# Transposing tokens by DMA between partitions and VectorE in 32 by 32 blocks, in place of TensorE, in a three-part decoder layer

## The chip, the cores and the metric

The kernel runs on one core of a Trainium2 chip. The metric is device time in microseconds (us). All rows of the profile come from one profiled execution; the kernel was also timed in three runs. TensorE is called PE in the profile, its weight loads PEld, VectorE DVE, ScalarE ACT, GpSimd POOL, and SyncE, which issues most DMAs, SP.

## The reference

One decoder layer in float32 for 4 batches of 1024 tokens with 512 features: gated self attention, cross attention to a context of 1024 x 384, and a small feed-forward network (FFN), each behind a layer norm and a residual. Both attentions have 16 heads of 32.

```python
# self attention, x normalized first (xn = layernorm(x))
inner, outer, v = heads(xn @ Wi), heads(xn @ Wo), heads(xn @ Wv)
a = softmax(inner @ outer.T / sqrt(32)) * sigmoid(xn @ Wa + ba)[query] * sigmoid(xn @ We + be)[key]
a = a / (a.sum(-1) + 1e-8)
x = x + rotate_and_gain(a @ v) @ Wout
# cross attention
q, k, v = heads(layernorm(x) @ Wq + bq), heads(ctx @ Wk + bk), heads(ctx @ Wv + bv)
x = x + (softmax(clip(q @ k.T / sqrt(32))) @ v) @ Wo + bo
# FFN: 64 channels, each through its own network of 16 hidden units
s = layernorm(x) @ Win + bin
g = sum_h(relu(s[..., None] * W1 + b1) * W2) + b2
x = x + g @ Wout + bout
```

## The kernel before

All time goes to `moderate_path`; `general_path` behind it runs only if a flag finds extreme values, and does not run here.

**Tiling.** A tile of tokens is [128 partitions, 512]. Half a batch is 4 such tiles (`xt` of [128, 4, 512], index `t`), a batch has two halves `hf`. A projection contracts over features, so normalized tokens, which lie with tokens on partitions, must be turned so that features lie on partitions. `tr(hf, t)` in `pre` does that: four `nc.tensor.transpose` of 128x128 (line 354) into one PSUM bank and a copy back over the tokens (`evacuate`, line 254 on ACT once attention has begun, line 258 on VectorE before). The `tr(t)` of `post` does the same (line 688) for the FFN's input. After that, chunk `c` of the features is `xn[:, :, ts(c, P)]`: 4 runs of 128 columns.

**Matmuls.** `columns` (line 86) splits each matmul with 128 output partitions into four of 32, which run abreast. Every float32 matmul shows as two PE instructions, a transpose as one.

**Passes.** `u` counts eight passes: phase 0 (self attention) for batches 0 to 3, then phase 1 (cross attention and FFN) for batches 0 to 3. `attention(u, hf)` gives 32 steps, 4 head groups `g` by 8 key tiles `kt`. A step computes scores for four heads (line 494), exponentials on ACT into the `e` tiles (line 499, two of six buffers a step), sums of `e` over key tiles on VectorE (`es`, lines 505 and 507; in phase 0 also `eg`, lines 514 and 515), and the `av` matmuls of the step before (line 521). Phase 0 and the last pass give part of the sums to TensorE (`shared`, line 529); passes 4 to 6 have two `es` additions of 128x1024 a step. At the end of a head group the sums go through small DMAs and DRAM: `add_up` (one step later) sends `sum_d` and `cs`, `divide` (two steps later) `rec_d` and four `recb` broadcasts to 32 partitions each, `multiply` (two more steps) needs them (line 601).

**Work beside the steps.** `pre(u)` holds the preparation of a pass (loads `x` or `ctx`, layer norm `ln`, transposes `tr`, projections `k`, `q`, `v`, gates `g` and `gt`), `post(u, hf)` what follows attention: loads, the output projection `o`, and in phase 1 layer norm, transposes and `inputs` (`s`), the hidden units `h` and `out`. `beside(u, hf)` writes out by hand, as a list, which of these runs next to which half: the preparation of pass u+1 and the post of the half before. Each entry has a load in units (one unit is a group of four matmuls of 512 columns abreast; a projection of one head group or one tile is 4 units, 3 from the context, and items with load 0 run as they are reached). `run` spreads the list so that the units are used up evenly over the 32 steps; `weave` mixes light items into heavy ones in a fixed proportion. On PE, VectorE, ACT and GpSimd the order of the program is kept; SP's DMAs are put in order by the framework's scheduler, and go out as their buffers come free.

**Buffers.** Tokens, context and the FFN's input share a pool `p3` of three buffers (`tok`). PSUM has two banks for everything that is no score and no accumulator (`bank()`). In phase 0 `r2` is one buffer between GpSimd and a store.

Of the kernel before, what the change touches and what calls it, by code (L numbers as in the profile page):

```python
# [16 lines left out]
P = 128  # L17
# [21 lines left out]
MAGIC = 0x5F3759DF  # L39

# [22 lines left out]
def moderate_path(tc: tile.TileContext, a: dict, out: bass.AP, flag: bass.AP):  # L63
    nc = tc.nc
    x = a["x"]
    with ExitStack() as st:
# [15 lines left out]
        def columns(to, lhsT, rhs, **flags):  # L82

            for j in range(4):
                r = slice(j * DH, (j + 1) * DH)
                nc.tensor.matmul(to[r], lhsT=lhsT[:, r], rhs=rhs, **flags)  # L86
# [7 lines left out]
        rec_d = [dram.tile([HG, HALF], F32, tag=f"rec_{i}", name="rec_d") for i in range(4)]  # L94
        wout_d = dram.tile([P, NC, D], F32, name="wout_d")
# [16 lines left out]
        def load_w(which):  # L112
            w = wp.tile([P, NC, D], F32, tag="w", name="w")
            if which == "o0":
                nc.sync.dma_start(w, wout_d)
            else:
                src, n = W_IN[which]
                nc.sync.dma_start(w[:, 0:n, :], src.rearrange("(c p) f -> p c f", p=P))
            return w

        x0 = p3.tile([P, 4, D], F32, tag="tok", name="xin")
        nc.sync.dma_start(x0, x[0].rearrange("(t p) d -> p t d", p=P)[:, 0:4, :])
        wae = const.tile([P, NC, 2 * H], F32, name="wae")
        nc.scalar.dma_start(wae[:, :, 0:H], a["attn_Wa"].rearrange("(c p) h -> p c h", p=P))
        nc.scalar.dma_start(wae[:, :, H:], a["attn_We"].rearrange("(c p) h -> p c h", p=P))
# [88 lines left out]
        nc.gpsimd.dma_start(win, a["ffn_Win"].rearrange("(c p) m -> p c m", p=P))  # L214
# [63 lines left out]

        order = [(ph, b) for ph in range(2) for b in range(B)]
# [15 lines left out]
        def pre(u):  # L295
# [4 lines left out]
            def load_ctx(hf):  # L300
                def f():
                    t = p3.tile([P, NC, HALF], F32, tag="tok", name="ctxT")
                    nc.sync.dma_start(
                        t[:, 0:NCK, :],
                        a["ctxT"][b].rearrange("(c p) t -> p c t", p=P)[:, :, hf * HALF : (hf + 1) * HALF],
                    )
                    me["ctx", hf] = lambda c: t[:, c, :]
                    me["ctx", hf, "t"] = lambda c, i: t[:, c, ts(i, P)]
                return f

            def load_x(hf):
                def f():
                    if u == 0 and hf == 0:
                        xt = x0
                    else:
                        xt = p3.tile([P, 4, D], F32, tag="tok", name="xin")
# [8 lines left out]
            def ln(hf):  # L325
# [14 lines left out]
                def norm(t):  # L340
                    def f():
                        xt = me["xn", hf][:, t, :]
                        normalized(xt, xt, res["mv"], res["rs"], t)
                    return [(0, f)]

                return [stats(t) for t in range(4)] + [[(0, root)]] + [norm(t) for t in range(4)]

            def tr(hf, t):
                def f():

                    xn = me["xn", hf]
                    tp = bank()
                    for c in range(NC):
                        nc.tensor.transpose(tp[:, ts(c, P)], xn[:, t, ts(c, P)], ident)
                    evacuate(xn[:, t, :], tp)
                    me["in", hf] = lambda c: xn[:, :, ts(c, P)]
                    me["in", hf, "t"] = lambda c, i: xn[:, i, ts(c, P)]
                return f
# [99 lines left out]
            def trs(hf):  # L458
                return [[(1, tr(hf, t))] for t in range(4)]
# [165 lines left out]
        def post(u, hf):  # L625

            ph, b = order[u]
            me = S[u]
# [43 lines left out]
            def root():  # L672
                i = 2 * NS + b * NT + 4 * hf
                nc.gpsimd.tensor_copy(marks[:, i : i + 4], res["mv"][:, :, 1])
                res["rs"] = rsqrt(res["mv"], 4)
                res["xn"] = p3.tile([P, 4, D], F32, tag="tok", name="xn")

            def norm(t):
                def f():
                    normalized(res["xn"][:, t, :], res[t], res["mv"], res["rs"], t)  # L680
# [3 lines left out]
            def tr(t):  # L684
                def f():
                    tp = bank()
                    for c in range(NC):
                        nc.tensor.transpose(tp[:, ts(c, P)], res["xn"][:, t, ts(c, P)], ident)  # L688
                    evacuate(res["xn"][:, t, :], tp)
                return f  # L690

            def inputs():
                ss = bank()
                for c in range(NC):
                    for j in range(4):
# [3 lines left out]
                            rhs=res["xn"][:, 2 * k : 2 * k + 2, ts(c, P)],  # L699
# [41 lines left out]
            if ph == 0:  # L741
# [5 lines left out]
                "s": [[(1, tr(t))] for t in range(4)] + [[(2, inputs)]],  # L747
# [38 lines left out]
        def beside(u, hf):  # L786

            last = post(u, 0) if hf else post(u - 1, 1) if u else None
            if u + 1 == n:
                out = last["load"] + pause(16) + last["o"] + weave(last["ln"], pause(4)) + pause(4)  # L790
                return out + last["s"] + weave(last["h"], pause(14)) + pause(2) + last["out"]
            p = pres[u + 1]
            next_ = pres[u + 2] if u + 2 < B else None
            if u + 1 < B:
                if hf == 0:
                    out = p["tr"][0] + p["x"][1] + p["k"][0][0:1] + p["g"][0] + p["k"][0][1:] + p["gt"][0]
                    if last:
                        out = last["load"] + out + weave(p["ln"][1], last["o"])
                    else:
                        out = one(rotations) + one(fold_bv) + out + [rotate(c) for c in range(NC)] + p["ln"][1]  # L800
                        out += [[(4, fold_bv)]]
                    return out + p["v"][0][0:1] + p["tr"][1] + p["v"][0][1:3] + p["g"][1] + p["v"][0][3:] + p["gt"][1]
                out = p["k"][1] + last["load"] + p["v"][1] + last["o"]
                if next_:
                    out += next_["x"][0]
                out += p["q"][0] + (weave(next_["ln"][0], p["q"][1][0:3]) if next_ else p["q"][1][0:3])
# [4 lines left out]
                return out + p["q"][1][3:]  # L811
            if hf == 0:
                out = p["ctx"][0] + p["ctx"][1] + last["load"] + p["k"][0]
                if "s" not in last:
                    return out + p["v"][0] + last["o"] + p["k"][1]
                out += p["v"][0][0:1] + last["o"] + weave(last["ln"], p["v"][0][1:2]) + p["v"][0][2:3] + last["s"]
                return out + weave(last["h"], p["v"][0][3:] + p["k"][1][0:3]) + p["k"][1][3:] + last["out"]
            if "s" not in last:
                out = last["load"] + p["v"][1][0:2] + p["x"][0] + p["v"][1][2:]
                out += p["x"][1] + weave(p["ln"][0], last["o"][0:3]) + last["o"][3:] + p["tr"][0]  # L820
                return out + p["q"][0][0:1] + weave(p["ln"][1], p["q"][0][1:]) + p["tr"][1] + p["q"][1]
            out = p["x"][0] + last["load"] + p["v"][1][0:1] + weave(p["ln"][0], p["v"][1][1:3]) + p["v"][1][3:]
            out += p["x"][1] + p["tr"][0] + p["q"][0][0:1] + weave(p["ln"][1], last["o"])
            out += weave(last["ln"], p["q"][0][1:2]) + p["q"][0][2:3] + last["s"]
            return out + weave(last["h"], p["q"][0][3:] + p["tr"][1] + p["q"][1][0:3]) + p["q"][1][3:] + last["out"]
# [3 lines left out]
        first += weave(p["ln"][1], p["q"][0]) + p["gt"][0] + p["tr"][1] + p["v"][0] + p["k"][1] + one(load_wout)  # L829
        first += p["g"][1] + p["q"][1] + p["gt"][1] + pres[1]["x"][0] + weave(pres[1]["ln"][0], p["v"][1])  # L830
# [667 lines left out]
```

## Time and profile before

| | us |
|---|---|
| median of three timed runs | 2300.78 (2300.62 to 2300.97) |
| the profiled execution | 2299.8 |
| its span, first to last instruction | 2298.0 |
| TensorE's granted clock, mean | 0.99 |

By parts of the span: 0 to 110 us prepare pass 0; the sixteen halves follow, 131 and 152 us in turn in phase 0 (128 and 140 in pass 3), 118 to 123 and 137 in phase 1, 113 and 111 in the last pass; from 2227.5 the post of the last half runs alone (70.5 us). A row of the groups gives line, engine, operation, output and inputs, shapes, count, then busy time in us and the mean of one in ns, then the engine's idle time before these instructions and what ended it. A row of the timeline gives start and length of merged instructions. A row of the windows gives a stretch, its length, then the busy time of each engine with its instruction count, the granted clock, the DMA engines' busy share and the GB/s moved.

### The profile page before, as it was taken

To read this page: it belongs to the slowest core of one execution; us is meant where nothing else is said; L and a number is where in the kernel's file an instruction comes from. 1 tells how busy PE (TensorE), PEld (TensorE's weight loads), DVE (VectorE), ACT (ScalarE), POOL (GpSimd) and SP (SyncE) were. 2 spreads that over 40 slices of the span, in tenths; PEclk is the share of its full clock that TensorE was granted. 3 is DMA by queue.
4 is the path that set the end of the run, shared out by engine and by line. 5 is a ranking of instruction groups with operands and counts; after the bars stand their busy time and mean duration, and the time that the engine had idled before them with its cause. 6 is when DMAs were issued, how large, how long until landed. Compare 5 with 4: busy or idle time off the path is not lost. (4 is left out here: it accounts for less than half of the span.)

```text
span 2298.0 us, 52871 instructions
## 1 busy us (share of the span) xinstructions
PE 2228.1 (97%) x22738; PEld 584.5 (25%) x22738; DVE 1528.2 (67%) x2401; ACT 1274.2 (55%) x1562; POOL 136.3 (6%) x143
## 2 busy tenths in 40 slices
PE   7999999999999999999999999999999999999984
PEld 2322222222222222222222222222222222222221
DVE  4368566775667756566865668678776878655554
ACT  0055545555455554555556565757576665757561
POOL 3000021000000000000000001000010101000100
PEclk9999999999999999999999999999999999999996
DMA  5202032120311203212311311202111221101010
GB/s 147 77 25 67 27 106 63 27 72 27 103 58 41 59 26 99 58 40 90 101 33 44 97 54 39 71 30 93 39 48 61 66 84 30 61 12 49 11 52 22
DMA packets 104021, 132.64 MB, mean 58 GB/s; under 512 B 44912, under 2 KB 45552, under 8 KB 102624
## 3 DMA queue, kind: packets, MB, share of 16 engines
q1 hardware_dynamic: 100464, 128.12, 18.0%
q8 instruction: 180, 2.95, 0.5%
q0 software_dynamic: 2000, 0.98, 0.3%
q14 instruction: 65, 0.53, 0.1%
q10 hardware_dynamic: 1312, 0.07, 0.0%
HBM read 101.00 MB, written 28.08 MB: 56 GB/s over the span
## 5 line engine op out<-in xcount | busy, mean ns | idle before, releaser
L499 ACT ACTIVATE e<-s 128x1024 f32<-128x1024 f32 x1024 | 994.2, 1023 | 719.3 <-PE s L494 526.4
L507 DVE TENSOR_TENSOR es<-es,e 128x1024 f32<-128x1024 f32 x528 | 645.6, 1246 | 331.5 <-ACT e L499 330.3
L494 PE MATMUL s<-q,k 32*64 32x512 f32 x8192 | 615.8, 613 | 6.2 <-ACT e L499 5.3
L521 PE MATMUL av<-e,v 128*32 128x512 f32 x4096 | 552.8, 604 | 0.0
L86 PE MATMUL f<-xin,w 128*32 128x512 f32 x3072 | 359.9, 596 | 4.7 <-ACT xin L254 3.9
L515 DVE SCALAR_TENSOR_TENSOR eg<-e,sw,eg 128x512 f32<-128x512 f32 x448 | 322.6, 756 | 2.3
L505 DVE TENSOR_TENSOR es<-e 128x1024 f32<-128x1024 f32 x88 | 115.4, 1334 | 234.0 <-ACT e L499 219.4
L86 PE MATMUL f<-w,q 128*32 128x512 f32 x2048 | 245.3, 598 | 10.0 <-DVE q L601 10.0
L494 PEld LDWEIGHTS s<-q,k 32*64 32x64 f32 x8192 | 136.0, 129 | 428.1 <-ACT e L499 208.6
L521 PEld LDWEIGHTS av<-e,v 128*32 128x32 f32 x4096 | 88.3, 108 | 403.6 <-issue 401.5
L86 PEld LDWEIGHTS f<-xin,w 128*32 128x32 f32 x3072 | 100.4, 110 | 233.3 <-issue 220.8
L529 PE MATMUL sm<-e,sw 128*2 128x512 f32 x1024 | 134.2, 596 | 0.0
L86 PE MATMUL f<-w,xin 128*32 128x512 f32 x1024 | 118.5, 592 | 0.7 <-DVE q L258 0.6
L661 POOL TENSOR_TENSOR r<-res,bo_bc 128x512 f32<-128x512 f32 x32 | 44.9, 1403 | 1124.4 <-DVE res L657 977.4
L86 PEld LDWEIGHTS f<-w,q 128*32 128x32 f32 x2048 | 67.4, 111 | 166.5 <-issue 149.9
L712 ACT ACTIVATE hid<-sT,units 128x256 f32<-128x256 f32 x128 | 72.0, 606 | 49.2 <-DVE sT L703 45.7
L86 PE MATMUL f<-ctxT,w 128*32 128x512 f32 x768 | 92.3, 592 | 0.0
L86 PE MATMUL f<-w,ctxT 128*32 128x512 f32 x768 | 91.7, 592 | 0.0
L718 DVE SCALAR_TENSOR_TENSOR g<-hid,units,g 128x256 f32<-128x256 f32 x120 | 57.9, 483 | 19.3 <-ACT hid L712 11.1
L551 PE MATMUL sm<-es,ones 128*1 128x512 f32 x352 | 68.2, 591 | 0.7 <-ACT both L540 0.7
L601 DVE TENSOR_TENSOR q<-both,recb 128x512 f32<-128x512 f32 x64 | 44.0, 687 | 27.7 <-DMA recb<-rec_d 27.4
L657 DVE TENSOR_TENSOR res<-f,res 128x512 f32<-128x512 f32 x64 | 44.0, 687 | 25.5 <-PE f L86 25.4
(231 smaller groups left out, 1081.2 us busy)
## 6 DMA issues: line engine op xcount, KB each, us to landing
recb<-rec_d SPq DMA_DIRECT2D x256, 64.0 KB
w<-in_xattn_Wo SPq DMA_DIRECT2D x9, 1024.0 KB
xin<-in_x SPq DMA_DIRECT2D x8, 1024.0 KB
res<-in_x SPq DMA_DIRECT2D x32, 256.0 KB
w<-wout_d SPq DMA_DIRECT2D x8, 1024.0 KB
x_d<-res SPq DMA_DIRECT2D x32, 256.0 KB
x1b_d<-r SPq DMA_DIRECT2D x32, 256.0 KB
xin<-x_d SPq DMA_DIRECT2D x32, 256.0 KB
```

The lines of the kernel that those rows point to most:

```text
L86: nc.tensor.matmul(to[r], lhsT=lhsT[:, r], rhs=rhs, **flags)
L494: nc.tensor.matmul(s[m : m + 64, j, :], lhsT=k[r, g, kt * P + m : kt * P + m + 64], rhs=q[r, g, :], start=True, stop=True,)
L499: nc.scalar.activation(e, s, AF.Exp, scale=SCALE)
L505: nc.vector.tensor_tensor(me["es"][i], me["e", 0][i], es[i], ALU.add)
L507: nc.vector.tensor_tensor(me["es"][i], me["es"][i], es[i], ALU.add)
L515: nc.vector.scalar_tensor_tensor(eg, es[0][:, h, :], gate(kt), eg, ALU.mult, ALU.add)
L521: nc.tensor.matmul(av[r, :], lhsT=me["v"][:, kt, HG * g + h, :], rhs=es[h // 2][:, h % 2, :], start=(kt == 0), stop=(kt == NT - 1),)
L529: nc.tensor.matmul(sm[j * DH : j * DH + sums, :], lhsT=me["sw"][:, t, HG * g + 2 + h, :] if ph == 0 else ones, rhs=me["e", t][1][:, h, :], ...
L551: nc.tensor.matmul(sm[j * DH : j * DH + 1, :], lhsT=ones, rhs=e, start=True, stop=True)
L661: nc.gpsimd.tensor_tensor(r2, r, bo_bc, ALU.add)
L712: nc.scalar.activation(hid, res["s"], AF.Relu, bias=units[:, 1, h : h + 1], scale=units[:, 0, h : h + 1])
L718: nc.vector.scalar_tensor_tensor(res["g"], res["hid"], units[:, 2, h - 1 : h], res["g"], ALU.mult, ALU.add)
```

## The change

Most transposes leave TensorE. They are split in two: DMAs move 32-row groups of tokens between partitions, and VectorE transposes 32x32 blocks in place.

- `spread` (15 of the 16 token sets, after the last norm of a set): 16 SP DMAs from the tokens (`tok`) to a second buffer `xT`; features of quarter `q` land on partitions 32q to 32q+31. `blocks` then transposes each [128, 512] tile on VectorE. In chunk `c`, partition 32q + i now holds feature 128q + 32c + i, and the chunk's columns lie in runs of 32 (`chunk`).
- Weights are loaded so that their rows match (`by_quarters`: four DMAs to 32 partitions each, for `q0`, `k0`, `v0`, `q1`, the gates' `wae` and the FFN's `win`).
- Before the FFN (7 of 8 posts), each norm writes to the one buffer `r2`, a DMA stores it to DRAM (`rows_d`), and after the fourth, four DMAs read the rows back in the spread order; then `blocks`.
- The first token set and the last post, where nothing runs beside, use `across`: 16 matmuls per tile against the identity, each 32 output partitions wide, into the same layout.
- Of the three `tok` buffers one stays for tokens and the FFN's input; two are now `inT`, for `xT`, the context and the first token set.
- `tr` items no longer count as load, and the lists of `beside` and of the start are written out anew so that other items stand between a spread and its `blocks`.

```diff
+NB = 32
             for j in range(4):
                 r = slice(j * DH, (j + 1) * DH)
-                nc.tensor.matmul(to[r], lhsT=lhsT[:, r], rhs=rhs, **flags)
+                nc.tensor.matmul(to[r], lhsT=lhsT[:, j, :] if len(lhsT.shape) == 3 else lhsT[:, r], rhs=rhs, **flags)
+        def by_quarters(dma, to, w):
+            for q in range(NC):
+                dma(to[ts(q, NB)], w[ts(q, P)].rearrange("(c i) f -> i c f", i=NB))
+        rows_d = [dram.tile([4, P, D], F32, tag=f"rows_{i}", name="rows_d") for i in range(2)]
...
+        def spread(to, xt):
+            for q in range(NC):
+                for s in range(P // NB):
+                    nc.sync.dma_start(to[ts(q, NB), :, ts(s, P)], xt[ts(s, NB), :, ts(q, P)])
+        def blocks(xt, t):
+            nc.vector.transpose(xt[:, t, :], xt[:, t, :])
+        def across(xt, t):
+            tp = bank()
+            for c in range(NC):
+                for q in range(NC):
+                    nc.tensor.matmul(
+                        tp[ts(q, NB), ts(c, P)], lhsT=xt[:, t, q * P + c * NB : q * P + (c + 1) * NB], rhs=ident,
+                        start=True, stop=True,
+                    )
+            to = xt[:, t, :].rearrange("p (s c j) -> p c s j", c=NC, j=NB)
+            evacuate(to, tp.rearrange("p (c s j) -> p c s j", c=NC, j=NB))
+        def chunk(xt, c, t0=0, n=4):
+            return xt[:, t0 : t0 + n, :].rearrange("p t (s c j) -> p (t s) c j", c=NC, j=NB)[:, :, c, :]
...
# pre: load_ctx, load_x, norm, tr
-                    t = p3.tile([P, NC, HALF], F32, tag="tok", name="ctxT")
+                    t = p2.tile([P, NC, HALF], F32, tag="inT", name="ctxT")
-                        xt = p3.tile([P, 4, D], F32, tag="tok", name="xin")
+                        xt = p1.tile([P, 4, D], F32, tag="tok", name="xin")
                         normalized(xt, xt, res["mv"], res["rs"], t)
+                        if xt0(hf):
+                            return
+                        if t == 3:
+                            me["xT", hf] = p2.tile([P, 4, D], F32, tag="inT", name="xT")
+                            spread(me["xT", hf], me["xn", hf])
-                    xn = me["xn", hf]
-                    tp = bank()
-                    for c in range(NC):
-                        nc.tensor.transpose(tp[:, ts(c, P)], xn[:, t, ts(c, P)], ident)
-                    evacuate(xn[:, t, :], tp)
-                    me["in", hf] = lambda c: xn[:, :, ts(c, P)]
+                    if xt0(hf):
+                        xn = me["xn", hf]
+                        across(xn, t)
+                    else:
+                        xn = me["xT", hf]
+                        blocks(xn, t)
+                    me["in", hf] = lambda c: chunk(xn, c)
-                return [[(1, tr(hf, t))] for t in range(4)]
+                return [[(1 if xt0(hf) else 0, tr(hf, t))] for t in range(4)]
...
# post: norm, tr
-                    normalized(res["xn"][:, t, :], res[t], res["mv"], res["rs"], t)
+                    if last:
+                        normalized(res["xn"][:, t, :], res[t], res["mv"], res["rs"], t)
+                    else:
+                        r2 = p1.tile([P, D], F32, tag="r2", name="r2")
+                        normalized(r2, res[t], res["mv"], res["rs"], t)
+                        nc.sync.dma_start(rows_d[hf][t], r2)
+                        if t == 3:
+                            for q in range(NC):
+                                nc.sync.dma_start(
+                                    res["xn"][ts(q, NB)].rearrange("j t (s f) -> j (t s) f", f=P),
+                                    rows_d[hf].rearrange("t (s j) f -> j (t s) f", j=NB)[:, :, ts(q, P)],
+                                )
+                return lambda: (across if last else blocks)(res["xn"], t)
...
# beside, the last pass, then phase 0, then phase 1 (hf 0, hf 1)
-                return out + last["s"] + weave(last["h"], pause(14)) + pause(2) + last["out"]
+                out = last["load"] + pause(16) + last["o"] + weave(last["ln"], pause(4)) + pause(4) + last["tr"]
+                return out + pause(2) + last["s"] + weave(last["h"], pause(14)) + pause(2) + last["out"]
+                    return out + v[0][0:2] + tr[1] + v[0][2:3] + p["g"][1] + v[0][3:] + p["gt"][1]
+                out = next_["x"][0] + k[1] + last["load"] + v[1] + last["o"] + weave(next_["ln"][0], q[0])
+                out += q[1][0:3] + next_["tr"][0] + q[1][3:]
+                out += k[0][0:3] + v[0][0:1] + last["o"] + weave(last["ln"], v[0][1:2]) + v[0][2:3] + last["tr"]
+                return out + v[0][3:] + last["s"] + weave(last["h"], k[1]) + k[0][3:] + last["out"]
+            out = x[0] + last["load"] + v[1][0:1] + weave(ln[0], v[1][1:3]) + v[1][3:] + x[1] + last["o"][0:1] + tr[0]
+            out += weave(ln[1], last["o"][1:])
+            out += weave(last["ln"], q[0][0:1]) + q[0][1:2] + tr[1] + last["tr"] + q[0][2:3] + last["s"]
+            return out + weave(last["h"], q[0][3:] + q[1][0:3]) + q[1][3:] + last["out"]
```

## The prediction

> **What bounds the kernel now.** I read the page first, for engine totals and the chain of work that ended last.
>
> ```profile
> PE 2228.1 (97%) x22738; PEld 584.5 (25%) x22738; DVE 1528.2 (67%) x2401; ACT 1274.2 (55%) x1562; POOL 136.3 (6%) x143
> ...
> PE 43%; ACT 2%; DVE 2%; issue 1%; DMA 1%; SPq 0%; DVEq 0%; ACTq 0%
> ```
>
> TensorE works 97% of the span and leads the chain; ACT has room everywhere. VectorE's 67% is a mean over unlike stages, so I cut the span at the ends of the 32-step halves (the copies of line 538 mark them): a phase-0 half with `hf`=0, then phase 1's `hf`=1 and `hf`=0 halves, and a half of the last pass.
>
> ```profile
> core 0: us, PE busy (x) PEld busy (x) DVE busy (x) ACT busy (x) POOL busy (x), PEclk, DMA share, GB/s
> 677.30:808.40 131.10, 131.10 (x1406) 35.00 (x1410) 97.72 (x156) 75.02 (x91) 7.06 (x5) 1.00 0.18 56
> 1346.50:1483.50 137.00, 134.40 (x1376) 37.29 (x1372) 106.48 (x169) 87.28 (x114) 7.54 (x5) 1.00 0.17 53
> 1483.50:1606.80 123.30, 122.88 (x1276) 31.82 (x1272) 92.68 (x121) 82.96 (x106) 6.63 (x5) 1.00 0.19 62
> 2003.60:2116.40 112.80, 112.19 (x1100) 27.11 (x1097) 62.82 (x96) 76.78 (x96) 6.75 (x5) 1.00 0.11 32
> ```
>
> The first two columns are the length and PE's busy time: PE is the limit in every half, at full clock (1.00). DVE comes nearest in phase 1's `hf`=1 (106.5 of 137).
>
> **What is removed.** 16 x 4 transposed tiles before projections and 8 x 4 before the FFN; tile sets (u=0, hf=0) and the last post stay on TensorE, so 60 + 28 = 88 tiles of four transposes go. Groups by line, then PE's timeline:
>
> ```profile
> L354 PE MATMUL f<-ident,xin 128*128 128x128 f32 x256 | 39.6, 293 | 17.0 <-DVE xin L277 13.4 <-ACT xin L254 2.6 <-DVE q L258 0.6
> L277 DVE TENSOR_SCALAR xin<-xin,bnmv,yi 128x512 f32<-128x512 f32 x64 | 32.8, 542 | 0.6
> L254 ACT COPY xin<-f 128x512 f32<-128x512 f32 x56 | 31.7, 596 | 6.4 <-PE f L354 6.4
> ```
> ```profile
> 1946.46 1.07 PE L521 MATMUL av<-e,v 128*32 128x512 f32 x8
> 1947.46 1.09 PE L688 MATMUL f<-ident,xn 128*128 128x128 f32 x8
> 1948.48 1.11 PE L494 MATMUL s<-q,k 32*64 32x512 f32 x16
> ```
>
> Where no transpose follows, the next group starts 0.88 us after `av` (1896.17 to 1897.05), so PE is free at 1947.34 and the next scores start at 1948.48: eight transposes hold it 1.14 us, a tile 0.57 us. 88 x 0.57 = 50 us. PE's idle time inside the halves is about 13 us (2.6 in each `hf`=1 half of u=4 to 6, 2.4 in the first half, the rest small), most of it right behind transposes that wait for ACT to empty one of two PSUM banks; I let 10 us go with them. **Gain 60 us.** The 84 ACT copies (0.6 us) that vanish were hidden by PE: nothing.
>
> **What is added, VectorE.** 88 block transposes of 128x512, in place in SBUF. No row shows one. Below: 481 ns (line 514, 512 elements); above: 1334 ns (line 505, 1024 elements). Nearest is line 277, one SBUF source, same shape, in place: 542; I take 0.6 us. They are 12 in a phase-1 `hf`=1 half: 106.5 + 7 of PE's 127; hidden in total, not in bursts (below). At the upper end they add 9 us more to each such half.
>
> The Trainium skill, "VectorE: DVE Perf Modes", section "The three transpose paths", gives VectorE 311 ns and TensorE 390 ns for 128x128 bf16 and advises TensorE for a full 128x128 since VectorE only turns 32x32 blocks. Four such blocks side by side would be an estimated 1.24 us a tile by that page, near my upper end; no row here shows it.
>
> **Added, strided operands.** Projections now read 16 runs of 32 columns as `rhs`. In before, 4 runs of 128 (`xin`) and one run of 512 (`ctxT`) have the same median of 592 ns, so runs cost nothing: I take 0. The slowest 512-column row, scores at 613, would bound it at 21 ns: 4096 matmuls, four abreast, 21 us. A gain has no ground: fewer runs gained none.
>
> **Added, transfers before projections.** 15 `spread`s of 16 DMAs, 64 KB each, in 512-byte pieces, 32 partitions to 32. SP issues such 32-partition DMAs 0.43 us apart (four `recb` in 1.72 us), and they move slowly; half-microseconds of a full-width load and of `recb` (last two columns: DMA share, GB/s):
>
> ```profile
> 1228.50:1229.00 0.50, 0.50 (x8) 0.13 (x4) 0.00 (x0) 0.50 (x3) 0.00 (x0) 1.00 1.06 414
> 1243.00:1243.50 0.50, 0.50 (x12) 0.17 (x8) 0.50 (x1) 0.50 (x1) 0.00 (x0) 1.00 0.61 107
> ```
>
> Bounds for 1 MB: issue alone 16 x 0.43 = 7 us; if each of 2048 packets took what a 2 KB `recb` packet took (0.61 x 16 x 0.5 us for 53 KB, 26 packets: 187 ns), 24 us. By bytes at 107 GB/s it is 10 us, which I take, the row being the nearest in shape.
>
> The skill's page "SBUF — State Buffer", section on the DMA port swizzle, says that 32 partitions reach 8 of 16 ports and lists 189 GB/s at 1 MiB. That is a rule against narrow DMAs and fits the slow `recb`; by it the transfer would be an estimated 5.5 us, under the issue bound.
>
> Cover: 10 us against, in phase 0, 8 units of later work at 52 units per 32 steps of 4.0 us (19 us), or 12 of 80 at 4.6 us (22 us, less one step while the buffer's last reader, the last part of `q[0]`, finishes). In phase 1: 8 of 66 units at 4.0 us (15.5 us), and `x[1]`, now in the same single buffer, loads behind it in 5 us, just as its statistics come up. Zero for these. While SP issues 16 DMAs, the sums, `rec_d` and `recb` of the division wait up to 7 us behind them; each leg has two steps (8 us) and uses about 4. Allowance 5 us. Uncovered, each spread would cost its 10 us.
>
> Weight loads in quarters: 48 more SP issues at 0.4 us in SP's idle time, prefetched; only the first, at 7.4 for 18.1 us, is near. `across` issues 32 matmuls where four transposes stood; line 398's 32 of that shape take 1.05 us, 0.5 us more a tile, for 4 tiles at the start and 4 at the end: 3 us with the first load. ACT's quarter loads are off the path.
>
> **Added, through DRAM before the FFN (7 posts).** Norms go to one `r2` buffer, each written out, then four reads. SP's timeline gives a write's landing, because the second line waits for the first:
>
> ```profile
> 1478.84 0.94 SPq L737 DMA_DIRECT2D out<-res  x2
> 1480.90 1.00 SPq L640 DMA_DIRECT2D res<-x1b_d  x2
> ```
>
> 2.06 us. `weave` puts norms 1 to 3 back to back (u=4 to 6), so two of them stand on VectorE for about 2.3 us each: the last is 4.6 late, plus a write 2.2 and reads 10: ready 17 us after its old place, with four blocks 19.4 (eight, with `tr[1]`: 21.8). Reads alone lie between 4 x 0.43 + 1 MB at 414 GB/s = 4 us and the 24 above.
> - u=5, 6, `hf`=0: 58 units, steps of 3.8 us: blocks stand 4 units behind (8.4 us), `inputs` 7 (14.7): PE waits 4.7, twice: 9.
> - u=4 to 6, `hf`=1: 66 units, 4.0 us: blocks 6 behind, `inputs` 10 (19.4): 2.4, three times: 7.
> - u=7: pauses part the norms; ready 12.2 + 2.4, `inputs` 7 of 64 units at 3.5 (12.2): 2.4, twice: 5.
> - Queued on VectorE behind a waiting block are the `es` additions; ACT has six `e` buffers, three steps, so about two steps (8 us) are swallowed. u=5's hold is 17 - 8.4 = 8.6, `hf`=1 adds norms and eight blocks: allowance 1.5 a post, 10.
>
> **Sum.** -60 + 5 + 3 + 9 + 7 + 5 + 10 = -21. The profiled execution took 2299.8 us, 1.8 more than its span and 1.0 under the median: 2299.8 - 21 = 2279.
>
> **Rivals.**
> 1. *Slower: the FFN's DRAM leg decides.* Each microsecond beyond 10 is paid in full at 7 posts, as PE already waits there. The remaining 21 us are gone at 13 us of transfer; that is the point. At 20 us: 7 x 10 = 70, and in four phase-1 `hf`=1 halves `x[1]` arrives 8 us late, half swallowed: 16. 2279 + 86 = 2365; at 16 us 2279 + 42 = 2321. For: 187 ns packets. Against: they were 2 KB, these 512 bytes.
> 2. *Everything hidden:* 2299.8 - 60 + 3 = 2243. For: VectorE idles over 20 us in most halves. Against: 8.4 us of cover for two chained transfers.
> 3. *VectorE binds in phase 1:* 1.3 us a transpose; 9 x 3 in `hf`=1 halves: 2306 at most; with half swallowed 2293. Against: line 277.
> 4. *The change doesn't take TensorE's work away:* strided reads give back 16 to 21 us: 2300, no change. Against: 592 twice.
>
> **How the numbers follow.** Forecast 0.54, its own range 2254 to 2295 (transfers of 7 to 12 us); rival 1 0.26; rival 2 0.12; rivals 3 and 4 0.04 each. About 0.2% (4.6 us) is what a measurement here can tell from no change. Faster: 0.54 less 0.03 for its edge, rival 2, and half of rival 3: 0.65; same: that edge, rival 4, and 0.02 of rival 1: 0.09; slower: 0.26. The range runs from rival 2's 2243 to 2330, past rival 1 at 16 us; about 0.15 lies above, 0.05 below.
>
> **What would show it.** Right: 384 transposes are gone and 256 short matmuls of `across` stand in for 32 of them (PE's count 22610), halves of phase 0 shorten by 4 x 0.57 us or a little more, and idle PE in phase 1 is behind line 697 (`inputs`), DVE's behind `rows_d` and `xT` DMAs. A spread should take about 10 us, a block transpose 0.6. Wrong: transposes over 1 us; `xin` matmuls over 592 ns; PE idle of 10 us or more a post; VectorE waiting for `xT` in phase 0; PE waiting for quarter-loaded weights.

## The result, and the profile after

The changed kernel takes 2357.85 us (median; 2356.2 to 2362.6) against 2300.74 before (here the median of four runs): ratio 1.0251, 95% interval 1.0234 to 1.0269. It is 2.5% slower; 2279, faster than before, was forecast, and 2330 was the upper end. The profiled execution took 2356.2, its span 2354.4. The same two rows of the page:

```profile
PE 2204.8 (94%) x22610; PEld 555.1 (24%) x22610; DVE 1558.0 (66%) x2485; ACT 1231.3 (52%) x1478; POOL 139.8 (6%) x146
...
PE 78%; DVE 7%; DMA 7%; SPq 3%; issue 2%; ACT 1%; DVEq 0%; ACTq 0%
```

TensorE's instruction count is the one forecast (22610) and it is busy 23 us less, yet the span grew by 56. DMA and SP's queue are 10% of the chain. (The shares of before add up to only 50% of the span, those of after to 98%, so the two chains can't be compared share by share.) Cutting at the copies of `av` again gives the place (us; "tiles" are the transposed tiles taken off TensorE, "best" is the last kernel of the experiments):

| | tiles | before | after | best |
|---|---|---|---|---|
| start and first half | 12 | 242.6 | 258.8 | 237.0 |
| phase 0, `hf`=0, u=1 and 2 | 16 | 262.2 | 257.2 | 257.2 |
| u=3, `hf`=1 | 8 | 140.0 | 142.9 | 137.8 |
| u=4 to 6, `hf`=1 | 36 | 410.6 | 425.2 | 393.5 |
| u=5 and 6, `hf`=0 | 8 | 246.6 | 259.3 | 240.8 |
| last pass | 8 | 223.9 | 238.7 | 221.6 |
| post of the last half | 0 | 70.5 | 70.6 | 68.8 |

The other halves (151.8 three times, 128.2, 118.1) kept their length. Between the start and the post of the last half TensorE's timeline after holds nine stalls of over 3.4 us; some of each kind (start, length, instruction; in brackets the idle time before it and what ended that):

```profile
117.08 3.31 PE L87 MATMUL f<-xT,w 128*32 128x512 f32 x16 [8.75 <-DMA w<-in_attn_Wo]
207.35 3.64 PE L87 MATMUL f<-w,xT 128*32 128x512 f32 x16 [15.98 <-DMA w<-in_attn_Wv]
1440.07 1.87 PE L594 MATMUL sm<-es,ones 128*1 128x512 f32 x4 [11.78 <-DVE es L550]
```

These are the second load of `Wo`, that of `Wv`, and the sums `add_up` of a head group in the `hf`=1 halves of u=4 to 6 (11.78, 10.75, 12.44). The other four are `inputs` (line 747), 3.9 to 5.3 each. All brackets over 0.5 us in this stretch add up to some 90 us, to 9 before. For the sums, the groups of before and after:

```profile
L551 PE MATMUL sm<-es,ones 128*1 128x512 f32 x352 | 68.2, 591 | 0.7 <-ACT both L540 0.7
```
```profile
L594 PE MATMUL sm<-es,ones 128*1 128x512 f32 x352 | 74.0, 620 | 36.7 <-DVE es L550 36.0
```

The `Wv` wait is explained on SP's timeline:

```profile
182.88 0.33 SPq L92 DMA_DIRECT2D w<-in_attn_Wv  x1
186.55 10.37 SPq L293 DMA_DIRECT2D xT<-xin  x16
197.01 0.56 SPq L600 DMA_DIRECT2D sum_d<-both  x1
197.62 1.05 SPq L605 DMA_DIRECT2D sum_d<-both  x2
198.71 0.44 SPq L92 DMA_DIRECT2D w<-in_attn_Wv  x1
...
204.21 0.43 SPq L92 DMA_DIRECT2D w<-in_attn_Wv  x1
```

Sixteen issues of a spread hold SP for 10.4 us, 0.65 each. With 3.3 us before them in which SP issues nothing, and the DMAs of the sums behind them, the second quarter of `Wv` goes out 16 us after the first and the fourth 21 us after it, 3.1 us before TensorE goes on. The third kind begins on VectorE, where the normalized tile waits for the one buffer `r2` (`rows_d<-r` is the store of the tile before):

```profile
1424.88 0.55 DVE L287 TENSOR_SCALAR r<-res,fmv,yi 128x512 f32<-128x512 f32 x1
1425.34 3.44 DVE L550 TENSOR_TENSOR es<-es,e 128x1024 f32<-128x1024 f32 x2
1432.10 0.55 DVE L287 TENSOR_SCALAR r<-res,fmv,yi 128x512 f32<-128x512 f32 x1 [3.32 <-DMA rows_d<-r]
1435.68 0.55 DVE L287 TENSOR_SCALAR r<-res,fmv,yi 128x512 f32<-128x512 f32 x1 [3.03 <-DMA rows_d<-r]
1438.34 0.55 DVE L287 TENSOR_SCALAR r<-res,fmv,yi 128x512 f32<-128x512 f32 x1 [2.11 <-DMA rows_d<-r]
1438.80 3.42 DVE L550 TENSOR_TENSOR es<-es,e 128x1024 f32<-128x1024 f32 x2
```
```profile
1418.08 11.41 SPq L293 DMA_DIRECT2D xT<-xin  x16
1429.59 0.54 SPq L729 DMA_DIRECT2D rows_d<-r  x1
```

The first norm is done at 1425.4, but its store goes out at 1429.59, behind the spread; then each norm stands for a store. The `es` addition of 1438.80, which TensorE's sums need, has been queued behind them.

Two things came as forecast. A block transpose takes 0.68 us (0.6 assumed) and strided operands cost nothing (596 ns as before):

```profile
L296 DVE STREAM_TRANSPOSE xT<-xT 128x512 f32<-128x512 f32 x60 | 37.3, 678 | 7.2 <-DMA xT<-xin 7.2
L87 PE MATMUL f<-xT,w 128*32 128x512 f32 x2816 | 334.5, 596 | 13.2 <-DMA w<-in_attn_Wo 8.8 <-DVE res L701 4.5
```

### The profile page after: what moved, and what is told of

It is laid out like the page before. It is cut to its first block, busy times and chain, and to the rows that moved or that the text cites. A ratio compares the mean times of both kernels' runs of the same rounds, so it can differ in the third digit from the quotient of the medians.

```text
span 2354.4 us, 53085 instructions
## 1 busy us (share of the span) xinstructions
PE 2204.8 (94%) x22610; PEld 555.1 (24%) x22610; DVE 1558.0 (66%) x2485; ACT 1231.3 (52%) x1478; POOL 139.8 (6%) x146
## 4 chain that ended last, share of the span: by engine, by line
PE 78%; DVE 7%; DMA 7%; SPq 3%; issue 2%; ACT 1%; DVEq 0%; ACTq 0%
PE f L87 30%; PE s L537 21%; PE av L564 17%; PE sm L572 5%; SPq L293 2%; DMA rows_d<-r 2%; PE sm L594 2%; DVE es L550 2%; ACT e L542 1%; DMA xn<-rows_d 1%; PE f L747 1%; PE f L779 1%; DVE r L287 1%; DMA sum_d<-both 1%; DVE bnst L368 0%
## 5 line engine op out<-in xcount | busy, mean ns | idle before, releaser
L87 PE MATMUL f<-xT,w 128*32 128x512 f32 x2816 | 334.5, 596 | 13.2 <-DMA w<-in_attn_Wo 8.8
L548 DVE TENSOR_TENSOR es<-e 128x1024 f32<-128x1024 f32 x88 | 108.0, 1247 | 194.8 <-ACT e L542 186.9
L87 PEld LDWEIGHTS f<-xT,w 128*32 128x32 f32 x2816 | 93.5, 111 | 228.1 <-issue 215.2
L87 PE MATMUL f<-w,xT 128*32 128x512 f32 x896 | 106.3, 601 | 16.5 <-DMA w<-in_attn_Wv 16.0
L594 PE MATMUL sm<-es,ones 128*1 128x512 f32 x352 | 74.0, 620 | 36.7 <-DVE es L550 36.0
```

Of the source, the lines that this page charges most:

```text
L87: nc.tensor.matmul(to[r], lhsT=lhsT[:, j, :] if len(lhsT.shape) == 3 else lhsT[:, r], rhs=rhs, **flags)
L548: nc.vector.tensor_tensor(me["es"][i], me["e", 0][i], es[i], ALU.add)
L594: nc.tensor.matmul(sm[j * DH : j * DH + 1, :], lhsT=ones, rhs=e, start=True, stop=True)
```

## The experiments

Theory A: the loss is waits at four places, made by SP's queue, one buffer, short leads and late rows. Theory B: the work that VectorE has taken over is what binds. Theory C, in the first four runs: the transfers themselves are slow, since their 512-byte pieces fill the DMA engines.

**The spread.** First one straight copy, then the same sixteen DMAs from another queue.

```diff
-            for q in range(NC):
-                for s in range(P // NB):
-                    nc.sync.dma_start(to[ts(q, NB), :, ts(s, P)], xt[ts(s, NB), :, ts(q, P)])
+            nc.sync.dma_start(to, xt)                                # e1_one_copy
+            # e4_pool_spread: the two loops, with nc.gpsimd.dma_start
```

> Each spread's 16 narrow DMAs are one full-width straight copy into the same buffer; block transposes and all waits stay, only the move between partitions is left out. Theory A (SP is held for 10 to 11 us by the 16 issues, and what stands behind them, weight quarters in pass 0 and the r2 stores in phase 1 hf=1, arrives late): PE's 16 us wait for Wv in pass 0 goes, the 11 to 12 us waits behind the es sums in phase 1 hf=1 shrink to about 5 (r2's own store waits stay): 2358 - 19 - 3 x 8 = about 2315. Theory B (VectorE is overfull in phase 1: 0.68 us transposes and r2 waits): phase 1 stays as it is, only pass 0 gains: about 2340. Theory C (the 512-byte pieces choke the DMA engines): like A.

> The 16 DMAs of a spread are issued by GpSimd in place of SP; same pieces, same bytes. This tells A from C. Theory A: SP is free, so Wv arrives in time in pass 0 (16 us wait gone) and the first r2 store no longer waits in phase 1 hf=1 (11 to 12 us waits down to about 6): 2315 to 2325 if GpSimd issues at its 0.55 to 0.6 us and its other work (line 705, 736) can wait. Theory C: the engines are as full as before and nothing changes beyond 10 us: 2348 or above. Theory B: pass 0 only, about 2340.

Measured: 2316.5 (ratio to before 1.0074, 1.0057 to 1.0091) and 2321.2 (1.0090, 1.0074 to 1.0107). Both are as A said, and C, which set the second at 2348 or above, falls. Moving the issue alone is worth 36.6 us of the 57; sending one DMA in place of sixteen adds only 5 more. So the spread's cost was mostly SP's time, not its narrow pieces (both runs move the same bytes, so neither prices those). With GpSimd TensorE waits 1.7 us ahead of the `Wv` projection, and the waits at the sums fall from about 12 to 8:

```profile
194.00 1.92 PE L87 MATMUL f<-w,xT 128*32 128x512 f32 x16 [1.69 <-DVE eg L558]
1415.88 1.87 PE L594 MATMUL sm<-es,ones 128*1 128x512 f32 x4 [8.00 <-DVE es L550]
```

**The rows' path.** Stores, reads and blocks of seven posts left out; `inputs` reads the last normalized tile.

```diff
-                        nc.sync.dma_start(rows_d[hf][t], r2)
-                        if t == 3: ...   # the four reads
+                        res["r2"] = r2
# ... (tr, the blocks, returns nothing)
-                            rhs=chunk(res["xn"], c, 2 * k, 2),
+                            rhs=chunk(res["xn"], c, 2 * k, 2) if last else res["r2"][:, 0 : 2 * P],
```

> The FFN's way through DRAM and its block transposes are left out in 7 posts: norms still go to r2, inputs reads r2 in place of the turned tokens. Theory A: without the stores behind the spread and without r2's waits, the 11 to 12 us PE waits of passes 4 to 6 hf=1 and the 4 to 5 us before inputs of passes 5 to 7 go, each with 1 to 2 us of slower clock behind it: 2358 - 3 x 13 - 4 x 6 = about 2295, pass 0 unchanged with its 16 and 9 us waits. Theory B: the same or less. Theory C (spreads themselves): only the 4 x 6 go, about 2335.

Measured: 2307.7 (1.0035, 1.0023 to 1.0048), so the path costs 50 us, 13 less than A had set. The halves of u=5 and 6 with `hf`=0 are 2.2 us shorter than before the change, but those of u=4 to 6 with `hf`=1 still wait at the sums, 5.4, 5.4 and 3.8 us, with no rows to wait for. There VectorE was busy without a pause from 1400 to 1437: the norms of `x[1]`, the blocks of `tr[0]` and the post's norms now lie close together. A had missed that B is right in these stretches (read from the timeline; no run moved these norms apart alone).

**The weight loads.** Full-width loads for the four quartered weights (rows then mismatched); then, as a single edit with nothing left out, only an earlier `Wo`.

```diff
-                    by_quarters(nc.sync.dma_start, w, src)      # e3_whole_weights: the full-width load
+        first += one(lambda: S[1].update(wk=load_w("k0")))      # e8_early_wo: ahead of p["v"][1]
```

> q0, k0, v0 and q1 load as one full-width DMA as before; the row order of the weights no longer matches the tokens, that part is left out. Theory A: in pass 0 a weight load is one issue that the spread can't split: the 16 us wait for Wv goes and the 9 us wait for Wo shrinks to 4 or less, each with its slow clock; later passes unchanged: about 2358 - 25 = 2333. Theory C: the waits in pass 0 are the DMA engines' backlog and stay at half or more: 2345 or above.

> The changed kernel with one edit: the second load of Wo is issued ahead of the first half's values, so that it takes a buffer that is free 15 us earlier. Theory A (narrow quarter loads take about 10 us, and only the lead decides): the 8.75 us wait at 117 us goes and the clock's loss behind it, 2347 to 2350. Theory B (the quarter loads share bytes per second with what else moves there): the wait shrinks by less than half, 2353 or more.

Measured: 2356.0 (1.0240, 1.0223 to 1.0257), a miss for A and in C's range, and 2352.3 (1.0224, 1.0204 to 1.0244), between A's 2350 and B's 2353. In the first TensorE no longer waits for `Wv`, but 4.9 us for exponentials a little later: VectorE stands still because the division's DMAs (`cs`), too, go out behind the spread.

```profile
212.42 0.19 DVE L615 TENSOR_TENSOR both__1646<-cs 128x32 f32<-128x32 f32 x1 [12.72 <-DMA cs<-sum_d]
```

Besides, the first projection started at 26.75 in place of 20.57, since VectorE waited for the gates' bias, loaded by ACT, and TensorE still waited 6.1 us ahead of the projection that reads `Wo`. (The profile names VectorE's rotations there, which that projection does not read; `Wo`'s one load had gone out 7.1 us before, at 115.96.) So that run does not price the quarter loads; it shows that SP's queue makes someone else wait when `Wv` does not. The second prices the lead of `Wo`: its wait fell from 8.75 to 1.78, and the stretch up to the end of the first half from 258.8 to 250.4.

```profile
109.50 1.92 PE L87 MATMUL f<-xT,w 128*32 128x512 f32 x16 [1.78 <-DMA w<-in_attn_Wo]
```

**VectorE's blocks**, left out alone (`blocks` does nothing):

> The changed kernel with the block transposes on VectorE left out (wrong tokens); all transfers stay. Theory A (VectorE's 0.68 us for each block transpose lie beside other work but in the four waits for the rows and in the three bursts of the second halves): about 2.7 us at each of these seven places, 2335 to 2343. Theory B (VectorE's added 57 us decide): 2315 or less.

Measured: 2360.7 (1.0260, 1.0244 to 1.0276), no gain at all: A's own price for them was too high, and B falls as the cause of the changed kernel's loss. The stalls at the sums stay as they were, and those at `inputs` now end with the transfer itself:

```profile
1444.69 1.87 PE L594 MATMUL sm<-es,ones 128*1 128x512 f32 x4 [11.86 <-DVE es L550]
1587.32 2.48 PE L747 MATMUL f<-xn,win 128*32 128x256 f32 x32 [3.52 <-DMA xn<-rows_d]
```

**The gain by itself**: one straight copy and no rows' path.

> Both kinds of movement are left out at once: the spread is one straight full-width copy, and the rows of seven halves take neither the DRAM leg nor the block transposes (both give wrong tokens); quarter weight loads and the blocks of the inputs stay. It measures the gain that the forecast put at 60 us. Theory A (the gain is there, the movement's waits ate it): the halves of the two single runs put together, 247.6 for the start, 128.6 in the middle halves, about 133 in the second halves of units 3 to 6, 121 in their first halves, 111.7 and 108.8 in the last unit, give 2265 to 2277; the forecast's own 60 us less a Wo wait of 6 would give about 2250. Theory B (VectorE's added block transposes bind): the blocks of the inputs stay, so 2285 or more, with waits for VectorE's sums in the second halves as long as before.

Measured: 2273.6 (0.9884, 0.9867 to 0.9900), as A. It keeps 5.4 us of waiting for `Wo` and 8.0 ahead of the `Wv` projection. Without these, and some 3 us for the slower clock behind them, it would be near 2257 (an estimate): a gain of some 40 us, not 60.

**Four places mended, nothing left out**, and the same with the spread on SP:

```diff
-                    nc.sync.dma_start(to[ts(q, NB), ...      # spread (e7_mended_sp keeps this line)
+                    nc.gpsimd.dma_start(to[ts(q, NB), ...
+        first += one(lambda: S[1].update(wk=load_w("k0")))
# ... (the projection then uses this load)
-                        r2 = p1.tile([P, D], F32, tag="r2", name="r2")
-                        normalized(r2, res[t], res["mv"], res["rs"], t)
-                        nc.sync.dma_start(rows_d[hf][t], r2)
+                        normalized(res["xn"][:, t, :], res[t], res["mv"], res["rs"], t)
+                        nc.sync.dma_start(rows_d[hf][t], res["xn"][:, t, :])
# beside: hf=0, hf=1, last pass (the post's ln, tr and s come later)
+                out += k[0][0:3] + v[0][0:1] + last["o"] + weave(last["ln"], v[0][1:2]) + v[0][2:]
+                out += [k[1][0][:1]] + last["tr"] + [k[1][0][1:]] + last["s"]
+            out += q[0][0:2] + weave(last["ln"], q[0][2:3]) + tr[1] + q[0][3:]
+            out += [q[1][0][:1]] + last["tr"] + [q[1][0][1:]] + last["s"]
+                out = last["load"] + pause(14) + last["o"] + weave(last["ln"], pause(4)) + pause(9) + last["tr"]
# ... (what follows in the three lists)
```

> All four places mended, nothing left out: GpSimd issues the spread, Wo's second load goes out ahead of the first half's values, the normalized rows go into the tile that the rows come back to (four slots in place of one), and blocks and inputs come 10 to 16 us later in the order of work. Theory A (the loss is waits for transfers at four places, with the clock's loss behind each): 2321 with GpSimd's issue alone, less 8 at Wo, less 28 at the sums of the second halves, less 32 at the inputs: 2250 to 2262, faster than the kernel before. Theory B (VectorE has become the bound in the second halves): its waits stay, about 2275 to 2290.

> As the mended kernel, but SyncE issues the spread as the change does. Theory A (SyncE's queue held for 11 us is a cost of its own): the 16 us wait for Wv stays, and the stores of the rows stand behind no spread any more, so 20 to 30 us over the mended kernel, 2272 to 2290. Theory B (only the order of the rows' work mattered): within 8 us of the mended kernel.

Measured: 2299.4 (0.9994, 0.9985 to 1.0004), a miss: slower than A's 2250 to 2262 and than B's 2275 to 2290; and 2322.7 (1.0098, 1.0078 to 1.0118), 23 us over it, as A says of SP: the `Wv` wait is 16.0 again. What was left in the first were short waits, at most 3.6 us: ahead of `inputs` (five times, 2.6 to 3.5), of query projections behind their blocks (2.2, three times), and of scores in the last pass (3.6 and 3.4):

```profile
1418.98 2.31 DVE L550 TENSOR_TENSOR es<-es,e 128x1024 f32<-128x1024 f32 x2
1423.47 0.69 DVE L644 TENSOR_TENSOR q<-both,recb 128x512 f32<-128x512 f32 x1 [2.18 <-DMA recb<-rec_d]
1424.08 4.62 DVE L550 TENSOR_TENSOR es<-es,e 128x1024 f32<-128x1024 f32 x4
1428.62 2.48 DVE L296 STREAM_TRANSPOSE xn<-xn 128x512 f32<-128x512 f32 x4
```

The reads went out at 1414.5 to 1416.4, and the blocks of 1428.62 wait for no transfer, but they stood behind 4.6 us of sums, and `inputs` had been put only one step after them: TensorE waited 3.1 us at 1429.97. The data was in time; VectorE's order was not.

**Blocks a step ahead, and the rows issued by GpSimd too**; then with one of the two undone, and with `r2` put back.

```diff
# on the mended kernel: e9_best
-                out += [k[1][0][:1]] + last["tr"] + [k[1][0][1:]] + last["s"]
+                out += last["tr"] + k[1][0:1] + last["s"]
-            out += q[0][0:2] + weave(last["ln"], q[0][2:3]) + tr[1] + q[0][3:]
-            out += [q[1][0][:1]] + last["tr"] + [q[1][0][1:]] + last["s"]
+            out += q[0][0:1] + [q[0][1][:1]] + weave(last["ln"], [q[0][1][1:], q[0][2][:1]]) + tr[1] + [q[0][2][1:]]
+            out += q[0][3:] + [q[1][0][:1]] + last["tr"] + [q[1][0][1:], q[1][1][:1]] + last["s"]
# ... (the last pass: one pause less before tr, two more behind it)
-                        nc.sync.dma_start(rows_d[hf][t], res["xn"][:, t, :])      # e10_best_sp_rows keeps this
+                        nc.gpsimd.dma_start(rows_d[hf][t], res["xn"][:, t, :])    # and the reads; bout added behind
# e12_best_one_r2: normalized(r2, ...) and the store from r2, as in the change
```

> The mended kernel, two things more, nothing left out: the blocks stand one step further ahead of the matmuls that read them, and the rows' stores and reads too are issued by GpSimd (its additions of bout behind them). Theory A (what is left are waits behind VectorE's own sums, by order only, and SyncE held by reads that wait for the stores, with the sums' transfers behind): of 2299.4 go 18 us at the inputs, 7 at the queries, 7 in the last unit and some 6 of lost clock: 2260 to 2275. Theory B (VectorE is full there whatever the order): the waits move to other matmuls, 2288 or more.

> As the last kernel, but SyncE issues the rows' stores and reads, as the change does. Theory A (the reads hold SyncE until the stores have landed, and the DMAs of the sums behind them come some 4 us later): 6 to 12 us over it, in the last unit above all. Theory B (who issues the rows does not matter once the order is right): within 3 us of it.

> The best kernel so far (2260), with one thing put back as the change has it: the norms before the FFN go through the one buffer r2, each store before the next norm, in place of the four slots of the tile that the rows come back to. Nothing is left out. Theory A (three norms stand on VectorE for a store each, 2 to 3 us, as in the changed kernel's rows, and what is behind them is late): rows 6 to 9 us later, PE waits for the rows or the sums, 3 to 6 us at each of seven posts: 2280 to 2300. Theory B (with nothing else held up, the six e buffers swallow it, as the forecast's allowance of 1.5 us a post supposed): 2260 to 2272.

Measured: 2260.2 (0.9831, 0.9817 to 0.9844), 2274.1 (0.9893, 0.9878 to 0.9908), and 2302.1 (1.0012, 1.0003 to 1.0022). The first holds A's figure and beats the kernel before by 39 us; from u=1 to the last half no stall of TensorE is over 2.4 us:

```profile
PE 2186.8 (97%) x22610; PEld 555.2 (25%) x22610; DVE 1569.8 (70%) x2485; ACT 1230.2 (54%) x1478; POOL 299.0 (13%) x442
```

SP as issuer of the rows costs 13.9 us, a little over A's range (with it GpSimd's additions of `bout` go back to their place behind each norm, so the figure is for both). In the mended kernel's last pass SP's rows show how, since the reads go out only when the stores have landed, and the sums' stores only after them:

```profile
2056.66 3.61 SPq L728 DMA_DIRECT2D rows_d<-xn  x4
2062.43 1.92 SPq L731 DMA_DIRECT2D xn<-rows_d  x4
2064.39 0.49 SPq L600 DMA_DIRECT2D sum_d<-both  x1
```

The single `r2` costs 42 us in the kernel where nothing else is held up, 2 more than A's upper end; B's 2272 at most, where the `e` buffers swallow the hold, is missed by 30. Two of its norms in the best kernel with `r2` put back:

```profile
1410.22 0.55 DVE L287 TENSOR_SCALAR r<-res,fmv,yi 128x512 f32<-128x512 f32 x1 [2.69 <-DMA rows_d<-r]
1415.33 0.55 DVE L287 TENSOR_SCALAR r<-res,fmv,yi 128x512 f32<-128x512 f32 x1 [4.56 <-DMA rows_d<-r]
```

## Why the prediction was wrong

The steps that failed are the cost of SP's queue, put at 5 us, the hold of the norms on VectorE's sums, put at 1.5 us a post, and the gain, a third of which did not come. The sum was -60 + 39; what the runs show is about -40 + 96. The best kernel moves all that the change moves, and its span is 39.6 us shorter than that of before and 96.0 shorter than that of the changed kernel. By the table 21.8 of the 96 lie in the start and first half, 36.8 in the `hf`=1 halves of u=3 to 6, 35.6 in the first halves of u=5 and 6 and the last pass, and 1.8 behind them. The prices below are from runs that take one cause away each; they overlap and do not add up. Two of the signs of being wrong that the prediction lists are there: TensorE waits for quarter-loaded weights (8.8 and 16.0 us), and 10 us or more a post (11 to 12 us, in three of seven).

- **Gain 60: about 40** (best kernel 39, and by estimate some 43 from the run that leaves the movement out). In the best kernel TensorE works 41 us less than before (2186.8 for 2228.1), where 50 was taken, and idles no less (71.6 for 69.9), where 10 was taken. A tile was priced at 0.57 us from a step with eight transposes. In a phase-0 half with `hf`=0 the profile of before has 32 transposes, eight tiles and not the four that the prediction's last part named, so 4.6 us by that price; the half shortened by 2.5. PE's groups in it, before and after:

```profile
L494 PE MATMUL s<-q,k 32*64 32x512 f32 x512 | 37.5, 613 | 0.0
...
L354 PE MATMUL f<-ident,xin 128*128 128x128 f32 x32 | 4.6, 281 | 0.0
```
```profile
L537 PE MATMUL s<-q,k 32*64 32x512 f32 x512 | 38.7, 613 | 0.3 <-ACT e L542 0.3
```

  The scores take 1.2 us more where the transposes are gone, and now wait for ACT: part of the freed time falls in steps with little other work, which the exponentials then pace (argued from these rows, not tried). The 10 us of idle time did not come on top. Of TensorE's waits inside the halves of before, 12.5 us in all, only 7.2 end with ACT's copies, so "most of it" was too much; the other 5.3 are scores that wait for exponentials. In the best kernel the first kind is gone, the second is 6.8, and 10.0 of other waits have come.
- **SP's collisions, 5: about 37.** This is the largest failure, a cost put almost at nothing (36.6 by the run that moves the issue to GpSimd). The issue was taken as 0.43 us from `recb`; a spread's took 0.65 to 0.72, 10.4 to 11.5 us together. More than its size, what stood behind it was missed: the prediction named the division's small DMAs, not `Wv`'s quarters (16 us of stall) nor the rows' first store. The division, which was named, does wait: VectorE stood 12.7 us for it in the run with whole weight loads. None of the four other halves of phase 0 that hold a spread got longer (151.8 us as before, or 2.5 shorter). The transfer itself, 10 us taken, ran at about 104 GB/s, near the 107 of the row it was priced by.
- **Weight loads, 0: about 8 at `Wo`** (start and first half 250.4 for 258.8 with the early load; 5.5 by the medians). "Only the first is near" was wrong: `Wo`'s second load gets its buffer at 107.35 and its four quarters take 9.7 us, with 1 us of other work ahead. Before, the transposes of `tr[0]` stood ahead of that projection, and it began 17 us after the load:

```profile
110.04 0.37 SPq L118 DMA_DIRECT2D w<-in_attn_Wo  x1
127.29 1.90 PE L86 MATMUL f<-xin,w 128*32 128x512 f32 x16
```

  The change took this lead away with them, and no term looked at it.
- **Rows, 9 + 7 + 5 + 10 = 31: 50.** The path was shorter than taken: in u=5's first half the last store goes out at 1571.89, the reads at 1574.43, and the blocks start at 1581.88, so 2.5 and 7.5 us, 10 in all for 12.2. Where no spread was in the way the term held: in u=5 and 6, `hf`=0, TensorE waits 3.9 and 4.2 us at `inputs`, 4.7 taken. In the `hf`=1 halves of u=4 to 6 it waits 11 to 12 us at the sums, where 2.4 was taken. There the lateness came ahead of the path: the store held by the spread, and the norms' stands, mostly 2.1 to 3.9 us each where 2.3 was taken. What failed is the allowance of 1.5 a post for the `es` additions queued behind: three steps of `e` buffers do not cover a hold of 14 us that ends at a head group's sums, where TensorE needs the last addition at once. The five terms were also added as if independent; the waits behind one another shifted from place to place as single ones were taken away (the second halves waited for 12, 8, 5 and 2.8 us at the same line).
- **The clock** was in no term. After a stall TensorE works at half its clock for some microseconds (last section); at about 2 us for each of nine stalls that is an estimated 18. The busy times are in line with it: the same 22610 instructions take 2204.8 us in the changed kernel and 2186.8 in the best one, 18.0 less. So TensorE's work shrank by 41.3 less 18.0, its idle time grew from 69.9 to 149.6, and 79.7 less 23.3 are the 56.4 that the span grew by.
- **Rivals.** The time lies where rival 1 had put a slower DRAM leg, but not for its reason: its break-even of 13 us of transfer was not reached (7.5 for the reads). Rival 3's VectorE does not bind in the kernel as changed (e11_no_blocks), and a block transpose takes 0.68 us and not the 1.3 it needed, though its bursts in `hf`=1 halves cost a few microseconds each once the rows are out of the way. Rival 2, all hidden at 2243, was missed by 115 us as the change stands; with another order and another issuer 2260 was reached. Rival 4 falls: the strided reads cost nothing.

## What to carry over

Before work is moved from a busy engine to DMAs, write down for every added DMA what the issuing queue holds behind it for that long, and who waits there: here the queue's time cost 37 us and sending one copy in its place saved only 5 more. Where an engine with strict order writes through a single buffer into a store, each further write stands for a whole store and everything behind it does too; give it as many slots as writes that come back to back. An operation that is off the critical path needs its place in the order as well as its data: here the last 39 us came from one step's distance and from who issued.

## What was not expected of the hardware

The granted clock falls while TensorE only waits, and stays down after it starts again. Windows of after around the `Wv` wait (the third figure from the end is the clock):

```profile
192.00:194.00 2.00, 0.00 (x0) 0.00 (x0) 1.08 (x2) 0.18 (x1) 0.00 (x0) 1.00 0.51 104
194.00:196.00 2.00, 0.00 (x0) 0.00 (x0) 0.00 (x0) 0.00 (x0) 0.00 (x0) 0.75 0.52 104
196.00:198.00 2.00, 0.00 (x0) 0.00 (x0) 0.00 (x0) 0.00 (x0) 0.00 (x0) 0.50 0.49 100
...
208.00:210.00 2.00, 2.00 (x16) 0.45 (x8) 0.00 (x0) 0.00 (x0) 0.00 (x0) 0.50 0.78 251
210.00:212.00 2.00, 2.00 (x24) 0.33 (x16) 0.00 (x0) 0.00 (x0) 0.00 (x0) 0.50 1.03 386
212.00:214.00 2.00, 2.00 (x32) 0.37 (x16) 0.31 (x1) 1.36 (x2) 0.00 (x0) 0.98 0.93 384
```

The last matmul before ended at about 191.4. The clock is 1.00 at 194 and 0.50 from about 195, and back some 4.7 us after the restart at 207.35; 4.7 us at half clock are 2.3 lost, and sixteen `columns` matmuls took 3.64 us for 1.90. The Trainium skill, "TensorE: Matmul & The Clock Gate", section "What's actually happening", gives a window of about 3.4 us for both turns, which agrees with these rows to about a microsecond. Yet the clock also fell after some stalls that were shorter than that window. In the best kernel it did so after 1.96 us, when TensorE had been at work again for 2 us, and stayed at half for about 3.4 us of work:

```profile
113.55 2.00 PE L537 MATMUL s<-q,k 32*64 32x512 f32 x16 [1.96 <-ACT e L542]
```
```profile
115.00:117.00 2.00, 2.00 (x16) 0.35 (x12) 1.93 (x5) 1.65 (x2) 0.00 (x0) 0.62 0.00 0
117.00:119.00 2.00, 2.00 (x16) 0.45 (x12) 2.00 (x3) 0.00 (x0) 0.00 (x0) 0.53 0.00 0
119.00:121.00 2.00, 2.00 (x28) 0.49 (x28) 0.94 (x2) 0.13 (x1) 0.00 (x0) 1.00 0.00 0
```

VectorE and GpSimd slow each other. In the best kernel, VectorE's four additions and GpSimd's four, side by side:

```profile
1411.46 8.90 DVE L550 TENSOR_TENSOR es<-es,e 128x1024 f32<-128x1024 f32 x4
```
```profile
1412.52 8.98 POOL L736 TENSOR_TENSOR res<-res,bout_bc 128x512 f32<-128x512 f32 x4
```

Each takes 2.2 us; four of VectorE's take 4.62, 1.16 each, when GpSimd is quiet (the mended kernel's rows above), and the median of GpSimd's is 1.29 in the best kernel. The Trainium skill, "SBUF — State Buffer", section "SBUF: two separate sides", describes a port pair that one of the two engines holds for a whole instruction, and fits. The same section warns that DMAs issued from GpSimd wait while VectorE runs an operation of a two-port mode, and advises another issuer. These runs show no such loss: in the best kernel GpSimd issued ten DMAs of a spread in 5.40 us, 0.54 each, where SP took 0.65 to 0.72, and what it waited for in the middle of some spreads (3.0 us in this one) was, by the profile, an earlier transfer of the same spread. A whole spread took it 8.7 to 12.2 us, and the kernel became faster by the move twice (36.6 and 23 us).
